# Layer-norm sums moved from TensorE to GpSimd in an RWKV block, with the raw weights on SyncE's queue

## The chip, the cores and the metric

The kernel runs on one core of one Trainium2 chip. The metric is device time in microseconds (us) of one execution; lower is better. A core has TensorE (PE, matrix products into the PSUM memory), VectorE (DVE), ScalarE (ACT), GpSimd (POOL) and SyncE (SP). Each engine takes its own instructions in order, and they wait for each other through semaphores. PE reads its operands from SBUF; DVE and ACT read SBUF or PSUM; GpSimd works on SBUF. Transfers (DMAs) are issued from the queues of SP, ACT and POOL.

## The reference

The input x has shape (2, 4096, 256): 2 sequences, 4096 time steps, 256 features.

```python
def _layernorm(x, axis=-1, eps=1e-05):
    m = jnp.mean(x, axis=axis, keepdims=True)
    v = jnp.var(x, axis=axis, keepdims=True)
    return (x - m) / jnp.sqrt(v + eps)

x = x + attention(_layernorm(x))
x = x + ffn(_layernorm(x))
```

The attention mixes each normalised time step with the one before it by three vectors, takes three products with 256x256 weights (k, v and r), runs a recurrence over time (a running log-maximum and a numerator with exponentials, the "wkv" scan), multiplies by sigmoid(r), and takes a product with W_o. The feed-forward part (ffn) takes two products from 256 to 1024 (w1, w2; silu of one times the other), two from 1024 to 1024 (h1, h2; gelu after each), and one back from 1024 to 256 (w3), each with a scale per output.

## The kernel before

Features lie on the 128 partitions and time along the free dimension; 256 features are two chunks. The work is cut into 16 tiles of 512 time steps, 8 for each sequence. A layer norm therefore sums across partitions.

**Products.** The ffn works in a split form: each operand is a pair (hi, lo), where hi is the value rounded to a shorter format (fp32r) and lo the remainder in the same format, and each product is two matmuls (`split_product`, lines 174 and 175). The attention's products are plain fp32 (`product`, line 167). After a product of the hidden layers ACT writes hi (L592) and the unrounded `full` (L594), and DVE subtracts them to give lo (L595). The next layer's products read both.

**The check of the weights.** The ffn's weights are kept as rounded copies. `compare` loads a raw piece of 128x512 values through GpSimd's queue (L154), and DVE compares it with the kept piece and counts differences (L156). There are 44 pieces: 28 of w1, w2, h1 and w3, and 16 of h2, which are compared while a block of h2 lies in SBUF. Where a difference is found, a second form of the whole block (`general_block`) runs after this one.

**The layer norm before.** `average` (lines 184 to 204) forms a mean over 256 features. DVE adds the two chunks (`both`, L189). ACT moves the upper 64 partitions down (`folded`, L191), DVE adds the lower 64 (L194), ACT rounds the result (`parts`, L196), and DVE puts the remainder into the other 64 partitions (L199). Then one matmul with a matrix of 1/256 sums over the partitions and gives the mean to every partition (L203). `layernorm` uses it twice: for the mean (then two subtractions, L214, and ACT's squares, L217) and for the variance (then ACT's square root, L220, DVE's reciprocal, L222, and two multiplications, L224).

**The order of the work.** The first tile has code of its own (`first_tile`), written out in order by `on`, `behind` and `last`. Then a loop runs `ffn(i)` as a generator of 26 steps (8 for w1 and w2, 8 for h1, 8 for h2, 2 for w3). Between its steps it takes pieces of two other generators: `attention(i + 1)`, which ends with the norm of x2 for the next ffn, and `normalise(i + 2)`, the first norm of the tile after. The piece of work at a step gives a scheduler its priorities; the scheduler then sets each engine's order, and an engine with nothing urgent that is ready is given later work (the mix operations, L304 and L305, of a later tile). `tc.issue_after` puts an instruction behind a named one.

**Buffers and queues.** The h2 blocks come from a copy in HBM through SP's queue (L588), three ahead. GpSimd's queue carries x in, the results out (L616), the raw pieces, and in the opening the rounding loads of the weights and the copies of h2 (L125). `ps_ffn` has four PSUM banks and `full` three buffers.

Of the kernel before, what the change touches and what calls it, by code (L numbers as in the profile page):

```python
# [2 lines left out]

# [4 lines left out]

F32 = mybir.dt.float32
# [56 lines left out]
def split_block(ctx, tc, flags, x, vecs, w_attn, w1, w2, h1, h2, w3, out):  # L66


    nc = tc.nc
    tensor, vector, scalar = nc.tensor, nc.vector, nc.scalar  # L70
# [61 lines left out]
    eps = const.tile([P, 1], F32, name="eps")  # L132
# [8 lines left out]
    numer = const.tile([P, ND], F32, name="numer")  # L141


    pieces = []
    for sb, src in ((w1_sb, w1), (w2_sb, w2), (h1_sb, h1), (w3_sb, w3)):
        n = src.shape[1] * src.shape[2] // PIECE
        sb, src = (t.rearrange("p a b -> p (a b)") for t in (sb, src))
        pieces += [(sb[:, k * PIECE : (k + 1) * PIECE], src[:, k * PIECE : (k + 1) * PIECE]) for k in range(n)]
    rounded = const.tile([P, len(pieces) + NH * (NH * P // PIECE)], F32, name="rounded")
    found = iter(range(rounded.shape[1]))  # L150

    def compare(kept, given, shape):
        raw = tmp.tile(shape, F32, tag="full", name="raw")
        nc.gpsimd.dma_start(out=raw, in_=given)  # L154
        j = next(found)
        vector.scalar_tensor_tensor(  # L156
            raw, raw, 1.0, kept.bitcast(F32), ALU.mult, ALU.not_equal, accum_out=rounded[:, j : j + 1]
        )

    def col(base, j):  # L160
        return vec[:, base + j : base + j + 1]
# [19 lines left out]
        marks["rounded"] = scalar.activation(hi, full, AF.Copy)  # L181
        marks["rest"] = vector.tensor_tensor(lo, full, hi.bitcast(F32), ALU.subtract)  # L182

    def average(a, b, tag, name, pause=False):

        both = one.tile([P, TS], F32, tag=tag, name="both")
        marks["both"] = vector.tensor_tensor(both, a, b, ALU.add)  # L189
        folded = one.tile([P // 2, TS], F32, tag="folded", name="folded")  # L190
        marks["shift"] = scalar.activation(folded, both[P // 2 :, :], AF.Copy)  # L191
        if pause:
            yield
        marks["fold"] = vector.tensor_tensor(folded, folded, both[: P // 2, :], ALU.add)  # L194
        parts = one.tile([P, TS], F32R, tag="parts", name="parts")
        marks["hi"] = scalar.activation(parts[: P // 2, :], folded, AF.Copy)  # L196
        if pause:
            yield
        marks["split"] = vector.tensor_tensor(parts[P // 2 :, :], folded, parts[: P // 2, :].bitcast(F32), ALU.subtract)  # L199
        if pause:  # L200
            yield
        psum = ps_sum.tile([P, TS], F32, tag="ps", name=name)
        marks["average"] = tensor.matmul(psum, mean_wr, parts, start=True, stop=True)  # L203
        return psum

    def layernorm(src, new_xc, tag, pause=False):


        mean = yield from average(src[:, 0, :], src[:, 1, :], tag, "mean", pause)
        if pause:  # L210
            yield
        xc = new_xc()
        for h in range(ND):
            vector.tensor_tensor(xc[:, h, :], src[:, h, :], mean, ALU.subtract)  # L214
        yield
# [5 lines left out]
        yield  # L221
# [53 lines left out]
    def normalise(i):  # L275

        x_sb = loaded.pop(i)
        if i + 1 < len(tiles):
            loaded[i + 1] = load_x(i + 1)
        xn = []  # L280

        def new_xn():

            xn.append(one.tile([P, ND, TS + 1], F32, tag="xn", name="xn"))
            if tiles[i][1] == 0:
                vector.memset(xn[0][:, :, 0:1], 0.0)
            else:
                vector.tensor_copy(xn[0][:, :, 0:1], prev)
            return xn[0][:, :, 1:]

        yield from layernorm(x_sb, new_xn, "rstd1", pause=i == 1)
        vector.tensor_copy(prev, xn[0][:, :, TS:])
        normal[i] = (x_sb, xn[0])

# [47 lines left out]
    def on(engine, operation, *args, **kwargs):  # L342
        with behind(engine):
            last[engine] = getattr(getattr(nc, engine), operation)(*args, **kwargs)  # L344
# [56 lines left out]
    def first_tile(second):  # L401
# [126 lines left out]
        last["vector"], last["scalar"] = marks["both"], marks["shift"]  # L528
# [35 lines left out]

    def ffn(i, x1, x2):

        checks = pieces[2 * (i - 1) : 2 * i] if i > 0 else []
        ha = []
        for f in range(NH):
            fs = slice(f * P, (f + 1) * P)  # L570
# [11 lines left out]
        for layer, scales in enumerate((SH1, SH2)):  # L582
            src, ha = ha, []
            for f in range(NH):
                fs = slice(f * P, (f + 1) * P)
                if layer == 1:
                    block = stream.tile([P, NH, P], F32R, tag="h2", name="h2_sb")
                    nc.sync.dma_start(out=block.bitcast(F32), in_=h2_hbm[f].bitcast(F32))  # L588
# [5 lines left out]
                scalar.activation(full, ps, AF.Gelu, scale=col(scales, f))  # L594
                vector.tensor_tensor(lo, full, hi.bitcast(F32), ALU.subtract)  # L595
                ha.append((hi, lo))
                if layer == 0 and f % 4 == 0 and checks:
                    compare(*checks.pop(), [P, PIECE])
                if layer == 1 and i == f + 1:
                    n = PIECE // P  # L600
                    for c in range(0, NH, n):
                        compare(block[:, c : c + n, :], h2[:, c : c + n, fs], [P, n, P])
                yield
        for h in range(ND):
            ps = ps_ffn.tile([P, TS], F32, tag="pf", name="po")
# [12 lines left out]
    def run(steps):  # L618
        for _ in steps:
            pass  # L620
# [8 lines left out]
        vector.tensor_scalar(inexact, everywhere, 0.0, None, ALU.is_gt)  # L629
        return inexact  # L630

    assert len(pieces) <= 2 * (len(tiles) - 1)
    normal, got = {}, {}
    second = normalise(1)
    first_tile(second)
# [2 lines left out]
    for i in range(len(tiles)):  # L638
        ahead = attention(i + 1) if i + 1 < len(tiles) else iter(())
        further = normalise(i + 2) if i + 2 < len(tiles) else iter(())  # L640
        for step, _ in enumerate(ffn(i, *got.pop(i))):
            if i == 0:
                if step in (0, 1, 2, 3, NH - 1):
                    with tc.issue_after(marks["rounded"].ins), tc.issue_after(marks["rest"].ins):
# [12 lines left out]
    return inexact[0:1, 0:1]  # L657


# [275 lines left out]
```

## Time and profile before

| What | Value |
|---|---|
| median of 3 runs | 1566.05 us (1565.85 to 1567.45) |
| the profiled execution's own time | 1567.88 us |
| its span | 1566.0 us |
| mean granted TensorE clock | 0.998 |
| one steady tile (332.2 to 427.9 us) | 95.7 us: PE busy 95.7, DVE 70.7, ACT 65.4, POOL 4.1 |

A row of a group reads: line, engine, operation, output<-inputs, sizes, count | busy us in total, mean ns of one | idle time of the engine just before, and what ended most of it. A row of the timeline reads: start us, duration us, engine, line, operation, and in brackets idle time before. Matmuls are pipelined and their ends are modelled, so the distance from start to start tells more of them than the duration does. GpSimd's spans are rough.

### The profile page before, as it was taken

The numbers are of one execution on the slowest core, as the hardware profiler recorded it, in microseconds if no ns is written. First come the engines' busy times: TensorE is split into PE (matmuls) and PEld (weight loads), VectorE is DVE, ScalarE is ACT, GpSimd is POOL, SyncE is SP. The second block draws the span as 40 slices with busy tenths as digits, with TensorE's granted clock in tenths as the row PEclk, the third lists the DMA queues.
The fourth block names the chain that finished last, engine by engine and source line by source line (L and its number), as shares of the span: only waits on it lengthen the run. The fifth ranks groups of instructions, "written<-read, shape, count | busy, mean of one in ns | idle before, by whom it ended". The sixth has DMA issues, their size and how long they took to land.

```text
span 1566.0 us, 16640 instructions
## 1 busy us (share of the span) xinstructions
PE 1555.8 (99%) x6313; PEld 1182.9 (76%) x6313; DVE 1102.0 (70%) x1763; ACT 1035.9 (66%) x1395; POOL 62.7 (4%) x100
## 2 busy tenths in 40 slices
PE   9999999999999999999999999999999999999998
PEld 6768777777777778777787777877777777777886
DVE  6788686776768767787676867767677676865531
ACT  5686757767577585776757766675776757756542
POOL 3000000000000000000000000000000000000000
PEclk9999999999999999999999999999999999999999
DMA  8612031120302204022030311203112030110302
GB/s 268 136 41 95 14 121 41 68 87 15 127 28 80 75 21 134 15 82 73 34 122 14 105 50 48 94 14 108 39 56 88 12 117 28 67 61 21 108 0 83
DMA packets 36886, 109.16 MB, mean 70 GB/s; under 512 B 3712, under 2 KB 12672, under 8 KB 36288
## 3 DMA queue, kind: packets, MB, share of 16 engines
q1 hardware_dynamic: 19424, 68.32, 13.1%
q0 software_dynamic: 16816, 39.07, 8.1%
q8 instruction: 51, 0.84, 0.2%
q10 hardware_dynamic: 560, 0.66, 0.1%
q14 instruction: 35, 0.29, 0.1%
HBM read 99.64 MB, written 12.58 MB: 72 GB/s over the span
## 4 chain that ended last, share of the span: by engine, by line
PE 98%; DVE 1%; ACT 0%; issue 0%; DVEq 0%
PE ph L174 30%; PE ph L175 30%; PE pa L174 4%; PE pb L174 4%; PE pb L175 4%; PE pa L175 4%; PE po L175 4%; PE po L174 4%; PE ps_k L167 3%; PE ps_r L167 3%; PE ps_v L167 3%; PE ps_o L167 3%; PE mean L203 1%; PE var L203 1%; PE ps_k L344 1%; DVE scale L344 0%
## 5 line engine op out<-in xcount | busy, mean ns | idle before, releaser
L174 PE MATMUL ph<-hi,h_sb 128*128 128x512 f32 x2048 | 813.5, 397 | 0.0
L175 PE MATMUL ph<-lo,h_sb 128*128 128x512 f32 x2048 | 801.0, 391 | 0.0
L174 PEld LDWEIGHTS ph<-hi,h_sb 128*128 128x128 f32 x2048 | 384.7, 188 | 93.5 <-issue 11.7
L175 PEld LDWEIGHTS ph<-lo,h_sb 128*128 128x128 f32 x2048 | 384.7, 188 | 89.1 <-issue 8.4
L592 ACT ACTIVATE hi<-ph,vec 128x512 fp32r<-128x512 f32 x256 | 175.7, 686 | 186.0 <-PE ph L175 184.5
L595 DVE TENSOR_TENSOR lo<-full,hi 128x512 fp32r<-128x512 f32 x256 | 175.5, 686 | 173.3 <-ACT full L594 172.2
L594 ACT ACTIVATE full<-ph,vec 128x512 f32<-128x512 f32 x256 | 174.3, 681 | 0.8 <-DVE lo L595 0.8
L577 DVE SCALAR_TENSOR_TENSOR gated<-pb,vec,gated 128x512 f32<-128x512 f32 x128 | 95.6, 748 | 57.6 <-PE pb L175 31.8
L592 ACT ACT_TABLE_LOAD x102 | 130.9, 1283 | 1.8
L576 ACT ACTIVATE gated<-pa,vec 128x512 f32<-128x512 f32 x128 | 86.6, 684 | 61.5 <-PE pa L175 58.3
L222 DVE RECIPROCAL rstd<-rstd 128x512 f32<-128x512 f32 x30 | 100.4, 3346 | 5.5 <-ACT rstd L220 5.5
L174 PE MATMUL pa<-x_hi,w_sb 128*128 128x512 f32 x256 | 101.9, 398 | 0.1
L174 PE MATMUL pb<-x_hi,w_sb 128*128 128x512 f32 x256 | 101.8, 398 | 0.0
L175 PE MATMUL pb<-x_lo,w_sb 128*128 128x512 f32 x256 | 100.6, 393 | 0.0
L175 PE MATMUL pa<-x_lo,w_sb 128*128 128x512 f32 x256 | 100.6, 393 | 0.0
L175 PE MATMUL po<-lo,w_sb 128*128 128x512 f32 x256 | 100.2, 392 | 0.0
L174 PE MATMUL po<-hi,w_sb 128*128 128x512 f32 x256 | 100.0, 391 | 0.0
L181 ACT ACTIVATE hi<-gated 128x512 fp32r<-128x512 f32 x128 | 80.6, 630 | 25.3 <-DVE gated L577 23.9
L182 DVE TENSOR_TENSOR lo<-gated,hi 128x512 fp32r<-128x512 f32 x128 | 87.8, 686 | 4.8 <-ACT hi L181 0.2
L250 DVE TENSOR_TENSOR_SCAN lm<-vec,lm,ps_k 128x512 f32<-128x512 f32 x30 | 38.3, 1278 | 44.2 <-PE ps_k L167 44.1
L305 DVE SCALAR_TENSOR_TENSOR mx<-xn,vec,mx 128x512 f32<-128x512 f32 x90 | 66.5, 745 | 0.3
L607 DVE SCALAR_TENSOR_TENSOR x_sb<-po,vec,x_sb 128x512 f32<-128x512 f32 x32 | 24.0, 751 | 59.0 <-PE po L175 59.0
(147 smaller groups left out, 1810.7 us busy)
## 6 DMA issues: line engine op xcount, KB each, us to landing
h_sb<-h_hbm SPq DMA_DIRECT2D x128, 512.0 KB, 3.2
raw<-in_h POOLq DMA_DIRECT2D x32, 256.0 KB, 3.1
x_sb<-in_x POOLq DMA_DIRECT2D x15, 512.0 KB, 4.0
out<-x_sb POOLq DMA_DIRECT2D x15, 512.0 KB, 3.1
h_sb<-in_h POOLq DMA_DIRECT2D x1, 4096.0 KB, 20.2
h_hbm<-in_h POOLq DMA_DIRECT2D x8, 512.0 KB, 12.7
w_sb<-in_w POOLq DMA_DIRECT2D x3, 1024.0 KB, 11.0
raw<-in_w POOLq DMA_DIRECT2D x12, 256.0 KB, 2.8
```

What stands on the lines that cost most here:

```text
L167: tensor.matmul(psum, weights(c), src[c], start=c == 0, stop=c == n - 1)
L174: tensor.matmul(psum, weights(c), hi, start=c == 0, stop=False)
L175: tensor.matmul(psum, weights(c), lo, start=False, stop=c == n - 1)
L181: marks["rounded"] = scalar.activation(hi, full, AF.Copy)
L182: marks["rest"] = vector.tensor_tensor(lo, full, hi.bitcast(F32), ALU.subtract)
L222: vector.reciprocal(rstd, rstd)
L305: vector.scalar_tensor_tensor(mx[:, h, :], xn[:, h, 1:], vec[:, j : j + 1], mx[:, h, :], ALU.mult, ALU.add)
L576: scalar.activation(full, pa, AF.Silu, scale=col(S1, f))
L577: vector.scalar_tensor_tensor(full, pb, col(S2, f), full, ALU.mult, ALU.mult)
L592: scalar.activation(hi, ps, AF.Gelu, scale=col(scales, f))
L594: scalar.activation(full, ps, AF.Gelu, scale=col(scales, f))
L595: vector.tensor_tensor(lo, full, hi.bitcast(F32), ALU.subtract)
```

## The change

- `average` becomes `total`: DVE adds the two chunks as before, and one GpSimd instruction, `partition_all_reduce`, sums over the 128 partitions and writes the sum to all of them, in SBUF. The folding, the rounding and the matmul go. The division by 256 moves into the subtraction and into the scale of the square root.
- The first norm's pieces are cut anew: sum; subtraction, squares and sum; square root, reciprocal and multiplications. These pieces (steps 12, 14 and 16) and the compares are issued after the latest hi, full and lo (`in_turn`). For tile 1 the pieces stand at steps 1 and 6 in place of 0, 1, 2, 3 and 7.
- A small `partition_all_reduce` in the opening makes GpSimd fetch the instruction's code there. A small add at the end, behind the last sum, brings back the usual code.
- Raw pieces are fetched through SP's queue, behind the latest h2 block, into one buffer, three steps before their compare; three pieces a tile, at steps 12, 16 and 20. The pieces of h2 are rounded again by ACT instead of being compared with the block in SBUF.

```diff
-    def average(a, b, tag, name, pause=False):
+    @contextmanager
+    def in_turn():
+        with tc.issue_after(marks["rounded"].ins), tc.issue_after(marks["rest"].ins):
+            yield
+
+    def total(a, b, tag):
         both = one.tile([P, TS], F32, tag=tag, name="both")
         marks["both"] = vector.tensor_tensor(both, a, b, ALU.add)
-        folded = one.tile([P // 2, TS], F32, tag="folded", name="folded")
-        marks["shift"] = scalar.activation(folded, both[P // 2 :, :], AF.Copy)
...
-        marks["fold"] = vector.tensor_tensor(folded, folded, both[: P // 2, :], ALU.add)
-        parts = one.tile([P, TS], F32R, tag="parts", name="parts")
-        marks["hi"] = scalar.activation(parts[: P // 2, :], folded, AF.Copy)
...
-        marks["split"] = vector.tensor_tensor(parts[P // 2 :, :], folded, parts[: P // 2, :].bitcast(F32), ALU.subtract)
...
-        psum = ps_sum.tile([P, TS], F32, tag="ps", name=name)
-        marks["average"] = tensor.matmul(psum, mean_wr, parts, start=True, stop=True)
-        return psum
+        everywhere = one.tile([P, TS], F32, tag="total", name="total")
+        marks["sum"] = nc.gpsimd.partition_all_reduce(everywhere, both, channels=P, reduce_op=ReduceOp.add)
+        return everywhere
...
-    def layernorm(src, new_xc, tag, pause=False):
-        mean = yield from average(src[:, 0, :], src[:, 1, :], tag, "mean", pause)
-        if pause:
+    def layernorm(src, new_xc, tag, spread=False):
+        mean = total(src[:, 0, :], src[:, 1, :], tag)
+        if spread:
             yield
         xc = new_xc()
         for h in range(ND):
-            vector.tensor_tensor(xc[:, h, :], src[:, h, :], mean, ALU.subtract)
-        yield
+            vector.scalar_tensor_tensor(xc[:, h, :], mean, -1.0 / D, src[:, h, :], ALU.mult, ALU.add)
+        if not spread:
+            yield
         sq = wide.tile([P, ND, TS], F32, tag="wide", name="sq")
         scalar.activation(sq, xc, AF.Square)
-        var = yield from average(sq[:, 0, :], sq[:, 1, :], tag, "var")
+        var = total(sq[:, 0, :], sq[:, 1, :], tag)
+        if spread:
+            yield
         rstd = one.tile([P, TS], F32, tag=tag, name="rstd")
-        scalar.activation(rstd, var, AF.Sqrt, bias=eps)
-        yield
+        scalar.activation(rstd, var, AF.Sqrt, bias=eps, scale=1.0 / D)
+        if not spread:
+            yield
         vector.reciprocal(rstd, rstd)
...
+    def fetch(j):
+        fetched[j] = stream.tile([P, PIECE], F32, tag="raw", name="raw", bufs=1)
+        with tc.issue_after(marks["block"].ins):
+            nc.sync.dma_start(out=fetched[j], in_=pieces[j][1])
+
+    def compare(j):
+        raw, kept = fetched.pop(j), pieces[j][0]
+        with in_turn():
+            if kept is None:
+                kept = tmp.tile([P, PIECE], F32R, tag="full", name="kept")
+                scalar.activation(kept, raw, AF.Copy)
+            vector.scalar_tensor_tensor(
+                raw, raw, 1.0, kept.bitcast(F32), ALU.mult, ALU.not_equal, accum_out=rounded[:, j : j + 1]
+            )
...
         load_table(AF.Exp)
         on("gpsimd", "tensor_copy", prev, xn[:, :, TS - 1 :])
+        on("gpsimd", "partition_all_reduce", root, eps, channels=P, reduce_op=ReduceOp.add)
...
+    steps = (NH + 4, 2 * NH, 2 * NH + 4)
...
             if step > 2 * NH - 6 and step % 2 == 0:
-                next(further, None)
+                with in_turn():
+                    next(further, None)
+            for k, at in enumerate(steps if i > 0 else ()):
+                j = (i - 1) * len(steps) + k
+                if j < len(pieces) and step in (at - 3, at):
+                    (fetch if step < at else compare)(j)
...
+    with tc.issue_after(marks["sum"].ins):
+        nc.gpsimd.tensor_tensor(root, eps, eps, ALU.add)
```

More of the change, by code (lines that the diff above doesn't have):

```diff
@@ L1 @@
 import math
-from contextlib import ExitStack, nullcontext
+from contextlib import ExitStack, contextmanager, nullcontext
 import concourse.bass as bass
@@ L7 @@
 from concourse._compat import with_exitstack
+from concourse.bass_isa import ReduceOp
 F32 = mybir.dt.float32
@@ L144, in split_block @@
     pieces = []
-    for sb, src in ((w1_sb, w1), (w2_sb, w2), (h1_sb, h1), (w3_sb, w3)):
+    for sb, src in ((w1_sb, w1), (w2_sb, w2), (h1_sb, h1), (w3_sb, w3), (None, h2)):
         n = src.shape[1] * src.shape[2] // PIECE
[L147 to L158, printed above, removed]
+        sb, src = (t if t is None else t.rearrange("p a b -> p (a b)") for t in (sb, src))
+        for k in range(n):
+            ks = slice(k * PIECE, (k + 1) * PIECE)
+            pieces.append((None if sb is None else sb[:, ks], src[:, ks]))
+    rounded = const.tile([P, len(pieces)], F32, name="rounded")
+    fetched = {}
+    def fetch(j):
[11 more added lines that the diff above has]
+            )
     def col(base, j):
@@ L182, in split @@
         marks["rest"] = vector.tensor_tensor(lo, full, hi.bitcast(F32), ALU.subtract)
-    def average(a, b, tag, name, pause=False):
+    @contextmanager
[3 more added lines that the diff above has]
+    def total(a, b, tag):
         both = one.tile([P, TS], F32, tag=tag, name="both")
         marks["both"] = vector.tensor_tensor(both, a, b, ALU.add)
-        folded = one.tile([P // 2, TS], F32, tag="folded", name="folded")
-        marks["shift"] = scalar.activation(folded, both[P // 2 :, :], AF.Copy)
-        if pause:
-            yield
-        marks["fold"] = vector.tensor_tensor(folded, folded, both[: P // 2, :], ALU.add)
-        parts = one.tile([P, TS], F32R, tag="parts", name="parts")
-        marks["hi"] = scalar.activation(parts[: P // 2, :], folded, AF.Copy)
-        if pause:
-            yield
-        marks["split"] = vector.tensor_tensor(parts[P // 2 :, :], folded, parts[: P // 2, :].bitcast(F32), ALU.subtract)
-        if pause:
-            yield
-        psum = ps_sum.tile([P, TS], F32, tag="ps", name=name)
-        marks["average"] = tensor.matmul(psum, mean_wr, parts, start=True, stop=True)
-        return psum
-    def layernorm(src, new_xc, tag, pause=False):
-        mean = yield from average(src[:, 0, :], src[:, 1, :], tag, "mean", pause)
-        if pause:
+        everywhere = one.tile([P, TS], F32, tag="total", name="total")
[4 more added lines that the diff above has]
+        if spread:
             yield
@@ L213, in layernorm @@
         for h in range(ND):
-            vector.tensor_tensor(xc[:, h, :], src[:, h, :], mean, ALU.subtract)
-        yield
+            vector.scalar_tensor_tensor(xc[:, h, :], mean, -1.0 / D, src[:, h, :], ALU.mult, ALU.add)
+        if not spread:
+            yield
         sq = wide.tile([P, ND, TS], F32, tag="wide", name="sq")
         scalar.activation(sq, xc, AF.Square)
-        var = yield from average(sq[:, 0, :], sq[:, 1, :], tag, "var")
+        var = total(sq[:, 0, :], sq[:, 1, :], tag)
+        if spread:
+            yield
         rstd = one.tile([P, TS], F32, tag=tag, name="rstd")
-        scalar.activation(rstd, var, AF.Sqrt, bias=eps)
-        yield
+        scalar.activation(rstd, var, AF.Sqrt, bias=eps, scale=1.0 / D)
+        if not spread:
+            yield
         vector.reciprocal(rstd, rstd)
@@ L289, in new_xn @@
             return xn[0][:, :, 1:]
-        yield from layernorm(x_sb, new_xn, "rstd1", pause=i == 1)
+        yield from layernorm(x_sb, new_xn, "rstd1", spread=True)
         vector.tensor_copy(prev, xn[0][:, :, TS:])
@@ L527, in first_tile @@
             next(second)
-        last["vector"], last["scalar"] = marks["both"], marks["shift"]
+        last["vector"] = marks["both"]
         banks = [
@@ L565, in ffn @@
     def ffn(i, x1, x2):
-        checks = pieces[2 * (i - 1) : 2 * i] if i > 0 else []
         ha = []
@@ L587, in ffn @@
                     block = stream.tile([P, NH, P], F32R, tag="h2", name="h2_sb")
-                    nc.sync.dma_start(out=block.bitcast(F32), in_=h2_hbm[f].bitcast(F32))
+                    marks["block"] = nc.sync.dma_start(out=block.bitcast(F32), in_=h2_hbm[f].bitcast(F32))
                 ps = ps_ffn.tile([P, TS], F32, tag="pf", name="ph")
@@ L593, in ffn @@
                 full = tmp.tile([P, TS], F32, tag="full", name="full")
-                scalar.activation(full, ps, AF.Gelu, scale=col(scales, f))
-                vector.tensor_tensor(lo, full, hi.bitcast(F32), ALU.subtract)
+                marks["rounded"] = scalar.activation(full, ps, AF.Gelu, scale=col(scales, f))
+                marks["rest"] = vector.tensor_tensor(lo, full, hi.bitcast(F32), ALU.subtract)
                 ha.append((hi, lo))
[L597 to L602, printed above, removed]
                 yield
@@ L630, in any_inexact @@
         return inexact
-    assert len(pieces) <= 2 * (len(tiles) - 1)
+    steps = (NH + 4, 2 * NH, 2 * NH + 4)
+    assert len(pieces) <= len(steps) * (len(tiles) - 1)
     normal, got = {}, {}
@@ L642, in split_block @@
             if i == 0:
-                if step in (0, 1, 2, 3, NH - 1):
-                    with tc.issue_after(marks["rounded"].ins), tc.issue_after(marks["rest"].ins):
+                if step in (1, NH - 2):
+                    with in_turn():
                         next(second)
@@ L651, in split_block @@
             if step > 2 * NH - 6 and step % 2 == 0:
-                next(further, None)
+                with in_turn():
+                    next(further, None)
[3 more added lines that the diff above has]
+                    (fetch if step < at else compare)(j)
             if i == len(tiles) - 1 and step == 3 * NH - 2:
```

## The prediction

> **What bounds the kernel now.** I read the page first (busy times, the chain that ended last), then the groups by line, then the timeline of PE and DVE around one norm. On the page:
>
> ```profile
> PE 1555.8 (99%) x6313; PEld 1182.9 (76%) x6313; DVE 1102.0 (70%) x1763; ACT 1035.9 (66%) x1395; POOL 62.7 (4%) x100
> ...
> PE 98%; DVE 1%; ACT 0%; issue 0%; DVEq 0%
> ```
>
> TensorE is busy everywhere and carries the chain. Its longest gap is 2 us in the opening. So only two things move the end: fewer slots on PE, or something that makes PE wait. A share of 70% on DVE is worth nothing by itself, but DVE is in order and hands PE its operands, so its order decides whether PE waits. The groups that the change touches:
>
> ```profile
> L203 PE MATMUL mean<-parts,mean_wr 128*128 128x512 f32 x30 | 18.5, 616 | 0.1
> L203 PE MATMUL var<-parts,mean_wr 128*128 128x512 f32 x30 | 17.9, 597 | 0.0
> L199 DVE TENSOR_TENSOR parts<-folded,parts 64x512 fp32r<-64x512 f32 x60 | 41.1, 685 | 31.0 <-ACT parts L196 30.1
> L194 DVE TENSOR_TENSOR folded<-folded,both 64x512 f32<-64x512 f32 x60 | 40.6, 678 | 1.4 <-ACT folded L191 1.4
> ...
> L344 POOL TENSOR_TENSOR mx<-mx 128x511 f32<-128x511 f32 x2 | 2.5, 1267 | 8.7 <-ACT mx L344 8.7
> ```
>
> Durations of matmuls overlap, so a matmul's price is read from starts. PE's timeline at the norm of x2, and after fp32 products with and without a sum between:
>
> ```profile
> 593.76 0.39 PE L174 MATMUL ph<-hi,h_sb 128*128 128x512 f32 x1
> 594.12 0.50 PE L203 MATMUL mean<-parts,mean_wr 128*128 128x512 f32 x1
> 594.46 0.40 PE L175 MATMUL ph<-lo,h_sb 128*128 128x512 f32 x1
> 594.70 0.39 PE L174 MATMUL ph<-hi,h_sb 128*128 128x512 f32 x1
> ```
>
> ```profile
> 565.72 0.79 PE L203 MATMUL mean<-parts,mean_wr 128*128 128x512 f32 x1
> 566.35 0.39 PE L174 MATMUL ph<-hi,h_sb 128*128 128x512 f32 x1
> ...
> 1426.88 0.79 PE L174 MATMUL ph<-hi,h_sb 128*128 128x512 f32 x1
> 1427.51 0.39 PE L175 MATMUL ph<-lo,h_sb 128*128 128x512 f32 x1
> ```
>
> The ordinary pitch is 0.23 us. The mean of x2 makes 0.36 + 0.34 = 0.70 us where one pitch would stand: 0.47 us. The mean of the first norm comes right after fp32 products; the 0.63 us behind it stands at 1426.88 too, where no sum is, so it belongs to the products and only one pitch, 0.23 us, is the sum's.
>
> **The change part by part.**
>
> *PE loses 60 matmuls.* A middle tile has four: 0.47 (mean of x2), about 0.26 (variance of x2, from its two gaps less a pitch), 0.23 and 0.23 (first norm). That is 1.2 us a tile, 15 norm pairs: **18 us**, all on the path.
>
> *DVE and ACT lose the folding.* DVE: L194 and L199, 41 + 41 = 82 us. ACT: L191 and L196, 120 copies of 0.63 us, 75 us. Neither is on the path; this is only room. Added: ACT rounds 16 pieces of h2 again (about 0.65 us each, 10 us), hidden by the ACT time freed. The mean's subtraction becomes a scalar_tensor_tensor, 0.75 for 0.68 us, 60 times, 4 us, hidden likewise. The 44 compares stay, three a tile instead of four in eight tiles and two in the rest.
>
> *Raw weights on SP.* 44 fetches of 256 KB with a landing of about 3 us, issued three steps (3.6 us each) before their compare: nothing. A fetch waits for the compare of the piece before (one buffer) and the h2 blocks queue behind it on SP; blocks are fetched three ahead, 11 us, and that compare stands at least one step earlier. Cover gone, a late compare would hold the block and so PE.
>
> *The opening.* POOL gets the code fetch and a dummy sum before its log_max and numer copies; these ended at 30.2 us because of DVE, the preceding copy at 16.0, so some 14 us are free; the Trainium skill (GPSIMD Engine Reference, Instruction dispatch) has about 6 us for a first call, and no row here shows one. The first real sum sits between the first and the other seven h2 copies, which so start after about 34 us plus a sum instead of 31.6. The first h2 block is asked for at 40.1, but products use it only from about 100 us. Nothing, if a sum is under some 20 us. At the end POOL's extra add and code switch lie beside the last 100 us of products: nothing. POOL also issues the out and x transfers; they stand behind the tile's last sum and start at the tile's end anyway.
>
> *The sums themselves.* 60 sums over partitions of 128x512 on POOL: nothing in the trace shows one. From below: the one 128x511 elementwise row, 1.27 us, which reads and writes the same tile without crossing partitions. From above: the Trainium skill (GPSIMD Engine Reference, Cross-partition) measured 247.7 us for a partition-axis reduce of [128, 2048]; a quarter is 62 us, an estimate, for a different instruction. At 62 us POOL alone would need 60 x 62 = 3720 us. I take 2.5 us, twice the near row, because a sum has to carry values between partitions and back where that row only streams them; call it X. Both ends stay in the range of cases below.
>
> What must cover X is DVE's work between the add (`both`) and the first use, in the built order, with DVE's pitches (0.6 for a 128x512 two-input operation, 0.65 with a scalar, 0.4 tensor_scalar, 3.3 reciprocal):
> - mean of the first norm: consumed two steps later, over 7 us.
> - variance of the first norm: the x_sb adds (waiting on products), a lo, a compare, a both, about 4.0; less the sqrt of 0.7: X up to 3.3.
> - mean of x2: reciprocal, lo, two multiplies: 3.3 + 0.6 + 1.2 = 5.1.
> - variance of x2: lo and five mix operations, 3.4, less sqrt and its hand-over 0.8: X up to 2.6.
>
> Behind each wait on DVE stand the next `lo` subtractions, and behind sqrt on ACT the next hi and full; `lo` is what PE's products read. Its slack now:
>
> ```profile
> 419.44 1.22 DVE L182 TENSOR_TENSOR x_lo<-x,x_hi 128x1024 fp32r<-128x1024 f32 x1
> 420.60 0.69 DVE L595 TENSOR_TENSOR lo<-full,hi 128x512 fp32r<-128x512 f32 x1
> ```
>
> ```profile
> 422.53 0.39 PE L175 MATMUL po<-lo,w_sb 128*128 128x512 f32 x1
> ...
> 426.43 0.39 PE L174 MATMUL pa<-x_hi,w_sb 128*128 128x512 f32 x1
> ```
>
> The last lo of a tile is ready at 421.3 and read at 422.5: 1.2 us. (x_lo, at 420.7, is read by the next tile from 426.4: 5.8 us.) So PE loses per tile (X - 3.3) + (X - 2.6) + (X - 5.1), each if positive, less 1.2. At X = 2.5 that is nothing; it starts at X = 3.6; it eats the gain of 1.2 us at 4.1; from there an extra us costs 30 and later 45 us of the whole. Sum at 2.5: 1567.9 (the profiled execution's own time; 1566.0 span) - 18 = 1549.9. That execution is 1.8 above the median 1566.05, so 1548 on the median's scale; I give **1549**.
>
> *The rule that speaks against it.* Row first: the two POOL rows of 1.27 us ran at 13.4 to 15.9 us beside DVE operations that read one operand from PSUM, and neither shows a delay; no row has POOL reading beside a two-input DVE operation. The Trainium skill (SBUF — State Buffer, Who interferes with whom) says that just this pair excludes each other: DVE with two SBUF inputs and a GpSimd instruction that reads SBUF share one interface, and the second waits until the first is done. Then the cover named above doesn't run: the lo, mix, compare and multiply operations have two SBUF inputs. What runs is the reciprocal and the PSUM adds. Per tile: (X - 1.6) + (X - 3.3) + X - 1.2, where positive. At X = 2.5: 0.9 + 0 + 2.5 - 1.2 = 2.2 us, 15 times 33 us, less 18: 1567.9 + 15 = 1583. So 1549 without the rule, 1583 with it, both at the same X; with it the gain survives only below X = 2.0. Whether this custom instruction holds the interface for its whole length or in short reads no run here shows; I put that at less than even.
>
> **The rivals.**
> 1. *The port lock* (slower). Place: DVE's lo and mix operations after the x2 variance add; price as above: X = 2: 1568; 2.5: 1583; 3: 1598; 4: about 1637. It decides from X = 2.0. For it: the rule; 66 us of DVE work a tile of 96. Against: no row.
> 2. *A long sum, no lock* (slower). Place: DVE's reciprocal of x2, which waits for sqrt, which waits for POOL. X = 5: (1.7 + 2.4 - 1.2) x 15 = 43, less 18: 1593; 6: 87 - 18: 1637; 10: about 1810. It decides from 4.1. For it: a sum across partitions does more per column than the 1.27 us row, and the other end is 62; against: nothing measured.
> 3. *Even.* The slots go and the waits give just that back: X near 4.1 without the lock or 2.0 with it: 1563 to 1569.
> 4. *The change doesn't free what it says*: if every gap after L203 belonged to the products, 60 x 0.23 = 14 us, 1554; still faster.
>
> **How the numbers follow.** A difference of 0.2%, 3 us, is about what a measurement here can tell from none. My case (18 us gained, a little given back, rival 4 included) 0.48, its own range 1545 to 1562; even 0.06; the lock 0.26; a long sum 0.20. Faster 0.48, same 0.06, slower 0.46. Below 1545 I see 3 in 100: nothing else leaves PE. Above, 1640 takes in the lock up to X = 4 and a long sum up to 6; beyond are some 15 in 100. Range 1545 to 1640.
>
> **What would show it.** Right: no L203 on PE, a period of 94.5 us a tile for 95.7, POOL rows of the sum near 2.5 us, DVE's reciprocal idle under 1 us before it, PE idle as before. The lock: lo and mix rows that start just when a sum ends, or rows as long as the sum. A long sum: reciprocal and subtraction idle with POOL or ACT rstd as releaser, PE idle before po with DVE lo as releaser, 4 gaps a tile. Code fetch: log_max copies late. Raw fetch: PE waiting for the DMA of an h2 block. If POOL's sum is over 4 us, or PE shows idle time in every tile, the forecast is wrong.

## The result and the profile after

The changed kernel takes 1571.28 us, the median of 8 runs (1569.6 to 1571.78); the kernel before, on the same chip, 1566.21 us. The ratio is 1.0029, with a 95% interval of 1.0018 to 1.004: slower by 0.3%, where 1549 was forecast, with a range of 1545 to 1640. The profiled execution took 1570.13 us, its span is 1568.3, and the granted clock was 1.0.

The page of the changed kernel, first its busy times and the chain that ended last, then groups by line (busy us, mean ns | idle before, releaser):

```profile
PE 1542.8 (98%) x6253; PEld 1171.0 (75%) x6253; DVE 1068.3 (68%) x1643; ACT 1030.7 (66%) x1334; POOL 238.6 (15%) x118
...
PE 69%; DVE 25%; ACT 4%; POOL 1%; issue 1%; POOLq 0%
...
L206 POOL PARTITION_ALL_REDUCE total<-both x60 | 202.0, 3367 | 920.1 <-DVE both L204 908.8
L603 DVE TENSOR_TENSOR lo<-full,hi 128x512 fp32r<-128x512 f32 x256 | 182.0, 712 | 193.1 <-ACT full L602 193.1
...
L186 PE MATMUL po<-lo,w_sb 128*128 128x512 f32 x256 | 103.7, 405 | 15.4 <-DVE lo L603 15.4
...
L312 DVE SCALAR_TENSOR_TENSOR mx<-xn,vec,mx 128x512 f32<-128x512 f32 x90 | 86.2, 982 | 0.0
```

TensorE has 60 matmuls fewer and is busy 13.0 us less, but the chain is no longer PE's alone: a quarter runs through DVE. PE now waits in front of `po` for `lo`. A mix operation (L312), which took 745 ns before, takes 982 ns on average. A sum takes 3.4 us on average.

The period, from the start of a tile's first `ps_k` to the next in PE's timeline, went from some 95.7 us to 96.4 in nine periods in a row and 95.5 in the last four (the one before these, next to the opening, is shorter in both kernels). Without the sums' matmuls it should have been 94.5. So about 2 us a tile are lost in most tiles. The timelines of GpSimd, DVE and PE in one of them (start, duration) show where:

```profile
489.72 3.23 POOL L206 PARTITION_ALL_REDUCE total<-both  x1 [18.00 <-DVE both L204]
493.89 3.23 POOL L206 PARTITION_ALL_REDUCE total<-both  x1 [0.94 <-DVE both L204]
502.94 3.53 POOL L206 PARTITION_ALL_REDUCE total<-both  x1 [5.82 <-DVE both L204]
```

```profile
491.35 1.16 DVE L603 TENSOR_TENSOR lo<-full,hi 128x512 fp32r<-128x512 f32 x1 [1.07 <-ACT full L602]
...
493.75 3.35 DVE L229 RECIPROCAL rstd<-rstd 128x512 f32<-128x512 f32 x1
...
503.30 2.73 DVE L312 SCALAR_TENSOR_TENSOR mx<-xn,vec,mx 128x512 f32<-128x512 f32 x1
505.95 1.19 DVE L311 TENSOR_SCALAR mx<-xn,unmix 128x512 f32<-128x512 f32 x2
507.06 1.40 DVE L312 SCALAR_TENSOR_TENSOR mx<-xn,vec,mx 128x512 f32<-128x512 f32 x2
508.39 3.34 DVE L229 RECIPROCAL rstd<-rstd 128x512 f32<-128x512 f32 x1
...
518.46 0.68 DVE L603 TENSOR_TENSOR lo<-full,hi 128x512 fp32r<-128x512 f32 x1
```

```profile
516.63 0.40 PE L185 MATMUL po<-hi,w_sb 128*128 128x512 f32 x1
517.27 0.50 PE L186 MATMUL po<-lo,w_sb 128*128 128x512 f32 x1 [0.24 <-DVE lo L603]
517.61 0.40 PE L185 MATMUL po<-hi,w_sb 128*128 128x512 f32 x1
519.20 0.50 PE L186 MATMUL po<-lo,w_sb 128*128 128x512 f32 x1 [1.19 <-DVE lo L603]
519.53 0.39 PE L185 MATMUL po<-hi,w_sb 128*128 128x512 f32 x1
```

The row of ACT that takes the result of the third sum:

```profile
506.50 0.73 ACT L226 ACTIVATE rstd<-total,eps 128x512 f32<-128x512 f32 x1 [3.41 <-POOL total L206]
```

The first two sums are those of the first norm's variance and of x2's mean; the third is x2's variance. Beside the third a mix operation takes 2.73 us, 2.0 more than its usual 0.74, and the pair of L311 behind it 1.19 for 0.87; beside the first a `lo` takes 1.16 for 0.69. The reciprocal that runs beside the second keeps its 3.35. After 491.35 DVE has no idle time until its last `lo`, so these delays stay in its queue: mix, mix, reciprocal, each later, and the last `lo` is done at 519.14. PE's four distances from 516.63 to 519.53 make 0.64 + 0.34 + 1.59 + 0.33 = 2.90 us where four pitches of 0.23 us make 0.92: 1.98 us lost, which is 96.4 - 94.4.

Three theories remain open at this point. The sum's reading of SBUF holds DVE up (the port lock: the two engines share a way into SBUF, and the second waits for the first). Or the sum is simply long, and what waits for it is late. Or DVE has too much in this window, mixes and comparisons ahead of the last `lo`, whatever GpSimd does.

### The profile page after: what moved, and what is told of

It reads as the page before. It is cut to its first block, busy times and chain, and to the rows that moved or that the text cites. A ratio compares the mean times of both kernels' runs of the same rounds, so it can differ in the third digit from the quotient of the medians.

```text
span 1568.3 us, 16558 instructions
## 1 busy us (share of the span) xinstructions
PE 1542.8 (98%) x6253; PEld 1171.0 (75%) x6253; DVE 1068.3 (68%) x1643; ACT 1030.7 (66%) x1334; POOL 238.6 (15%) x118
## 4 chain that ended last, share of the span: by engine, by line
PE 69%; DVE 25%; ACT 4%; POOL 1%; issue 1%; POOLq 0%
PE ph L185 18%; PE ph L186 18%; DVE rstd L229 6%; DVE mx L312 5%; DVE lo L603 4%; PE pa L185 4%; PE pb L185 4%; PE pa L186 4%; PE pb L186 4%; PE ps_k L178 3%; PE ps_v L178 3%; PE ps_r L178 3%; PE ps_o L178 3%; DVE mx L311 3%; PE po L186 3%; PE po L185 2%
## 5 line engine op out<-in xcount | busy, mean ns | idle before, releaser
L185 PE MATMUL ph<-hi,h_sb 128*128 128x512 f32 x2048 | 823.0, 402 | 0.6 <-ACT hi L192 0.6
L186 PE MATMUL ph<-lo,h_sb 128*128 128x512 f32 x2048 | 810.1, 397 | 0.0
L206 POOL PARTITION_ALL_REDUCE total<-both x60 | 202.0, 3367 | 920.1 <-DVE both L204 908.8
L603 DVE TENSOR_TENSOR lo<-full,hi 128x512 fp32r<-128x512 f32 x256 | 182.0, 712 | 193.1 <-ACT full L602 193.1
L186 PE MATMUL po<-lo,w_sb 128*128 128x512 f32 x256 | 103.7, 405 | 15.4 <-DVE lo L603 15.4
L312 DVE SCALAR_TENSOR_TENSOR mx<-xn,vec,mx 128x512 f32<-128x512 f32 x90 | 86.2, 982 | 0.0
L186 PEld LDWEIGHTS po<-lo,w_sb 128*128 128x128 f32 x256 | 48.0, 188 | 37.8 <-DVE lo L603 28.3
```

Of the source, the lines that this page charges most:

```text
L185: tensor.matmul(psum, weights(c), hi, start=c == 0, stop=False)
L186: tensor.matmul(psum, weights(c), lo, start=False, stop=c == n - 1)
L206: marks["sum"] = nc.gpsimd.partition_all_reduce(everywhere, both, channels=P, reduce_op=ReduceOp.add)
L312: vector.scalar_tensor_tensor(mx[:, h, :], xn[:, h, 1:], vec[:, j : j + 1], mx[:, h, :], ALU.mult, ALU.add)
```

## The experiments

All twelve were timed against the kernel before, whose median was between 1566.0 and 1566.8 us.

| Kernel | Median us | Ratio to before (95%) | Period of the middle tiles |
|---|---|---|---|
| sums that nobody reads, added to the kernel before | 1618.79 | 1.0333 (1.0319 to 1.0347) | 99.0 |
| one memset for each sum | 1545.98 | 0.987 (0.9855 to 0.9885) | 94.4 |
| six memsets for each sum | 1546.96 | 0.9876 (0.9861 to 0.9891) | 94.4 |
| three ordinary additions for each sum | 1574.38 | 1.0048 (1.0034 to 1.0061) | 95.7, later 98.6 |
| sum over half the columns | 1549.85 | 0.9895 (0.9879 to 0.991) | 94.6 |
| mixes moved | 1547.05 | 0.9875 (0.986 to 0.989) | 94.4 |
| comparisons moved | 1565.21 | 0.9993 (0.9985 to 1.0001) | 95.7 |
| both moved | 1548.01 | 0.9884 (0.9869 to 0.9899) | 94.4 |
| mixes moved in the kernel before | 1570.05 | 1.0023 (1.0016 to 1.003) | 96.0 |
| x2's variance back on TensorE | 1562.44 | 0.9971 (0.9961 to 0.9981) | 95.2 |
| the same, both moved | 1562.81 | 0.9976 (0.9968 to 0.9985) | 94.9 |
| both sums of x2 back, both moved | 1569.96 | 1.0028 (1.0018 to 1.0039) | 95.7 |

**Sums that nobody reads.**

```diff
         var = yield from average(sq[:, 0, :], sq[:, 1, :], tag, "var")
+        marks["sum"] = nc.gpsimd.partition_all_reduce(sq[:, 0, :], sq[:, 1, :], channels=P, reduce_op=ReduceOp.add)
```

> The kernel before, unchanged in its own sums over the channels, with 30 GpSimd sums of 128x512 added that nobody reads: one half of each squared tile is summed over the partitions into the other half, which is dead by then (two sums a tile, at the place of the two variances; the small one that fetches the code in the opening and the small addition at the end are there too). So the latency of the sum is on no path; only what it does to VectorE's access to SBUF can cost. Port lock: VectorE's lo or mix operations beside a sum grow by about 2 us each, the last lo before po is late in part of the tiles, and the time is 1570 to 1580 for 1566.2. Latency of the sum, or its place in VectorE's order: 1566 to 1567, and the lo and mix rows keep their 686 and 745 ns.

It took 1618.79 us, 52 us more than before and far more than I had expected of any theory. Its timelines of GpSimd, DVE and PE, and PE's waits (total us, times, longest):

```profile
397.53 3.23 POOL L220 PARTITION_ALL_REDUCE sq<-sq  x1 [19.66 <-DVE both L190]
```

```profile
397.82 2.50 DVE L598 TENSOR_TENSOR lo<-full,hi 128x512 fp32r<-128x512 f32 x1 [0.46 <-ACT full L597]
```

```profile
398.93 0.39 PE L175 MATMUL ph<-hi,h_sb 128*128 128x512 f32 x1
400.37 0.51 PE L176 MATMUL ph<-lo,h_sb 128*128 128x512 f32 x1 [1.05 <-DVE lo L598]
```

```profile
PE var L204 <- DVE parts L200: 27.8, 17, 1.9
PE ph L176 <- DVE lo L598: 14.0, 13, 1.4
```

Nothing depends on these sums, and no other engine waits for GpSimd's work in this trace; still a `lo` beside one takes 2.5 us and PE waits for it. The sum acts on DVE by being there, not by its result. In this kernel each blocked operation stands just ahead of what PE needs next: `lo` of the running product, and `parts`, for which the matmul of the variance waits in PE's own queue. PE's waits in the two rows make 41.8 of the 52 us; the kernel before has neither. So the same 2 us cost more here than in the changed kernel.

**Writes in place of the sum.** One memset, then six, which are as long as the sum (the edit of the six; the other has no loop):

```diff
-        marks["sum"] = nc.gpsimd.partition_all_reduce(everywhere, both, channels=P, reduce_op=ReduceOp.add)
+        for _ in range(6):
+            marks["sum"] = nc.gpsimd.memset(everywhere, 100.0)
```

> The changed kernel with each GpSimd sum replaced by one GpSimd memset of the 128x512 result: the sum itself is left out, so the norms are wrong, while every other instruction, TensorE's 60 matmuls fewer among them, is that of the changed kernel. Port lock or latency: the whole loss is the sum's, PE idle before po goes below 2 us in all, and the time is 1549 to 1553 for 1571.3. Backlog: if the compares and mix operations placed ahead of the last lo make it late by themselves, the time stays above 1560 with lo as PE's releaser before po.

> The changed kernel with each sum replaced by six GpSimd memsets of its 128x512 result, together about as long as the sum (some 3 us) but reading nothing: the sum is left out, the norms are wrong, its latency stays. Port lock by the sum's reading: no lo or mix row is prolonged and the time is that of the single memset, within 3 us (1549 to 1555). Latency: the time stays at 1567 to 1571, with reciprocal and subtraction late as in the changed kernel. If the memsets hold VectorE up as well, rows of 2 us and more show it, and the run cannot tell the two apart.

1545.98 and 1546.96 us, 3 and 2 us below the ranges given: without the sum's reading the whole loss is gone. The kernel with six memsets, its chain and groups:

```profile
PE 98%; DVE 1%; ACT 0%; issue 0%
...
L207 POOL MEMSET total<- 128x512 f32 x360 | 194.5, 540 | 972.1 <-DVE xn L218 771.6
```

```profile
L313 DVE SCALAR_TENSOR_TENSOR mx<-xn,vec,mx 128x512 f32<-128x512 f32 x90 | 65.3, 736 | 0.0
```

Six of 0.54 us are 3.2 us for each sum (3.4 to 3.6 from start to end in the timeline), and the mix keeps its 736 ns. Writes of the sum's length don't hold up the operations that its reading holds up. But memsets read nothing, so they don't wait for `both` either. At x2's variance they start 2.5 us before it:

```profile
491.38 3.61 POOL L207 MEMSET total<- 128x512 f32 x6 [2.94 <-DVE x L218]
```

```profile
493.86 0.67 DVE L204 TENSOR_TENSOR both<-sq 128x512 f32<-128x512 f32 x1
```

So this kernel doesn't keep the wait for the result, as its expectation had it, and doesn't decide on the second theory. The changed kernel's trace does more for that. At the place shown, the square root is done at 507.23 and DVE comes to the reciprocal at 508.39 without idle time: it doesn't wait for the sum. In the whole execution DVE waits 4.0 us for the square root and 3.4 for a sum. ACT waits 45.3 us for sums, 3.41 of them here, but DVE has no idle time behind it, so no `lo` was late for that. What the length alone would have cost there is an estimate: without the delays of 2.0 and 0.3 us DVE would have come at some 506.1, and without its own 0.3 us the sum would have let the square root end at 506.9, so 0.9 us would have shown.

How much of a delay DVE can bear, the kernel with one memset shows. From the `lo` behind DVE's idle time to the last `lo` of the tile, its DVE has the same operations as the changed kernel's, a mix and a pair of L311 in another place, and PE's order is the same. The last `lo` and the matmul that reads it:

```profile
507.61 0.69 DVE L603 TENSOR_TENSOR lo<-full,hi 128x512 fp32r<-128x512 f32 x1
```

```profile
509.13 0.39 PE L186 MATMUL po<-lo,w_sb 128*128 128x512 f32 x1
```

The `lo` is done 0.8 us before it is read. DVE takes 25.1 us for the stretch here and 27.8 in the changed kernel: 2.7 more, less 0.8, is 1.9, about what PE loses. So mixes and comparisons ahead of the last `lo` cost nothing by themselves, which ends the third theory alone, and the estimated 0.9 us of length would have gone nearly whole into the slack. By this reckoning the blocking is nearly all of the loss. (With six memsets DVE's order differs more: the last two mixes stand behind the last `lo`.)

**Ordinary reads in place of the sum.**

```diff
-        marks["sum"] = nc.gpsimd.partition_all_reduce(everywhere, both, channels=P, reduce_op=ReduceOp.add)
+        for _ in range(3):
+            marks["sum"] = nc.gpsimd.tensor_tensor(everywhere, both, both, ALU.add)
```

> The changed kernel with each sum replaced by three ordinary GpSimd additions of its input to itself, each reading the 128x512 tile and writing the result, about 1.27 us each by the row of 128x511, 3.8 us together; the sum over the partitions is left out, so the norms are wrong. It asks whether reading SBUF is enough, or whether it is the special instruction that holds VectorE up. Reading: mix operations of 1.5 to 4 us beside these rows, PE waiting before po for lo, 1562 to 1580. The special instruction alone: no row is prolonged, and the time is that of the writes, 1545 to 1550.

1574.38 us, and ordinary reading is enough to hold DVE up. The rows of GpSimd and DVE at x2's variance:

```profile
500.45 3.78 POOL L207 TENSOR_TENSOR total<-both 128x512 f32<-128x512 f32 x3 [5.00 <-DVE both L204]
```

```profile
501.81 1.52 DVE L313 SCALAR_TENSOR_TENSOR mx<-xn,vec,mx 128x512 f32<-128x512 f32 x1
503.25 1.52 DVE L604 TENSOR_TENSOR lo<-full,hi 128x512 fp32r<-128x512 f32 x1
```

A mix and a `lo` take 1.52 us here, 0.8 more than usual and less than one addition (1142 ns on average): DVE gets in between the additions, as if the two engines took turns. The three additions take 3.78 us here and 3.27 beside a reciprocal. The time itself proves less than the rows, since PE's order differs in some places too: 1.3 us a tile are lost in the middle (95.7 - 94.4) and 4.2 in the last tiles. Why more there stays open.

**Half of the columns.**

```diff
-        marks["sum"] = nc.gpsimd.partition_all_reduce(everywhere, both, channels=P, reduce_op=ReduceOp.add)
-        return everywhere
+        half = TS // 2
+        marks["sum"] = nc.gpsimd.partition_all_reduce(
+            everywhere[:, :half], both[:, :half], channels=P, reduce_op=ReduceOp.add
+        )
+        return everywhere[:, :half].unsqueeze(1).to_broadcast([P, 2, half])
...
```

> The changed kernel with each GpSimd sum taken over 256 of the 512 columns and used for both halves, so the second half of each norm is wrong; VectorE and ScalarE still work on all 512 columns. The sum is shorter (1.6 to 2.0 us by half of 3.24 and a start). Port lock in proportion to what is read: the blocked lo and mix rows fall from 2.5 to 2.9 us to 1.5 to 1.8, about half of the 24.6 us between the changed kernel (1571.3) and the one with writes only (1547.0) goes: 1555 to 1563. A fixed price for each sum whatever it reads: 1568 to 1571, rows as long as before.

1549.85 us: some 3 of the 24 us stay (1546.96 with writes only), where I had expected half, and the range that I gave is missed. At x2's variance, GpSimd and DVE:

```profile
496.70 2.09 POOL L207 PARTITION_ALL_REDUCE total<-both  x1 [7.34 <-DVE both L204]
```

```profile
497.05 1.59 DVE L319 SCALAR_TENSOR_TENSOR mx<-xn,vec,mx 128x512 f32<-128x512 f32 x1
```

The mix loses 0.85 us instead of 2.0, in proportion as expected, but PE then loses only 0.2 us a tile (94.6 - 94.4). The first part of a delay is taken up by the slack of the last `lo` (0.8 us with one memset); only what exceeds it reaches PE. The sum is also shorter here, so this run alone doesn't divide the gain between the two.

**Moving what stands beside the sum.** All sums stay on GpSimd. The mixes of the next tile go from the window of the x2 norm to the first steps of the next pass; the comparisons go to earlier steps.

```diff
+            if i > 0 and step in (1, 3, 5):
+                with in_turn():
+                    next(ahead, None)
-            for _ in range(0 if step < NH else 4 if step == NH + (i == 0) else 1):
+            for _ in range(0 if step < NH else 4 if i == 0 and step == NH + 1 else 1):
                 next(ahead, None)
```

```diff
-    steps = (NH + 4, 2 * NH, 2 * NH + 4)
+    steps = (4, NH, NH + 4)
```

> The changed kernel with only the three mix pieces of the next tile moved out of the window of the x2 norm, to product steps 1, 3 and 5 of the next pass; the comparisons stay at steps 12, 16 and 20. The mixes are 12 operations, 7.4 us, of the window's filler, and it is they that are prolonged to 2.7 to 2.9 us beside the sum of x2's variance; the two comparisons there are 1.2 us. If the mixes are what makes the lock cost: a period of 94.4 to 94.7 and 1547 to 1553, near the run with both moves (1548.0). If the comparisons matter as much: 1555 to 1565.

> The changed kernel with only the comparisons moved, to product steps 4, 8 and 12; the mix pieces stay in the window of the x2 norm. If the mixes are what makes the lock cost, little is won: VectorE has 1.2 us less to do ahead of the last lo, so PE's wait before po (1.4 us a tile at most) shrinks but mixes of 2.7 us remain: 1558 to 1570. If the comparisons are the cause: 1547 to 1555.

> The changed kernel, all four sums of a tile on GpSimd, with the filler moved out of the window of the x2 norm: the three mix pieces of the next tile's inputs at product steps 1, 3 and 5 of the next pass, the comparisons at steps 4, 8 and 12. The lock then meets only lo operations there, one a product step of 7.2 us, with nothing in VectorE's queue between them but the norm. Lock plus backlog: a lo grows by 2 us, but the last lo before po has that much room: PE's idle time before po falls below 5 us (43.7 in the changed kernel over matmuls and weight loads), the period to 94.4 to 94.8 and the time to 1547 to 1554. Lock whatever stands there: a blocked lo makes PE wait in any case: 1562 to 1571. Mixing late could make ps_k wait for mx in the next pass; then PE shows that, 1555 to 1575.

1547.05 us with the mixes moved, 1565.21 with the comparisons moved, 1548.01 with both. The mixes are what makes the lock cost: moved alone, they win back all of it, and the changed kernel becomes 1.25% faster than the one before. The comparisons ahead of the last `lo` are worth 6 us as long as the mixes stand there, and nothing after. With the mixes moved, GpSimd and DVE at x2's variance, and the chain:

```profile
496.43 3.53 POOL L206 PARTITION_ALL_REDUCE total<-both  x1 [4.98 <-DVE both L204]
```

```profile
496.18 0.69 DVE L603 TENSOR_TENSOR lo<-full,hi 128x512 fp32r<-128x512 f32 x1
500.75 3.35 DVE L229 RECIPROCAL rstd<-rstd 128x512 f32<-128x512 f32 x1 [3.89 <-ACT rstd L226]
```

```profile
PE 98%; DVE 1%; ACT 1%; issue 0%
```

The sum now lies beside nothing but the end of a `lo`. DVE stands idle for 3.89 us while it and the square root run, which looks worse in a share of busy time, and the end comes 24 us earlier. The lock is still there: `lo` takes 722 ns on average, where 682 is its mean without reads. It has just nothing queued behind it that is short of time.

**The move alone.** The same three steps in the kernel before, whose sums stay on TensorE.

> The kernel before with the move of the three mix pieces alone (product steps 1, 3 and 5 of the next pass), its sums on TensorE as they were. If the move is worth something by itself, it is faster than 1566: down to 1560, by L203's matmuls waiting less for the folding. If it is only a cure for the lock: 1565 to 1568, or slower where the folding of x2, with no filler between, is no longer the limit but the matmuls' place in PE's order is: up to 1580.

1570.05 us, 0.2% slower than before. So the move is no gain of its own, as the second reading had it, and slightly worse; it is the cure of what the sums on GpSimd bring.

**Sums given back to TensorE.** x2's variance as before, then with both moves, then both sums of x2 with both moves. The edit of the first, which also brings back `average`:

```diff
-        var = total(sq[:, 0, :], sq[:, 1, :], tag)
         if spread:
-            yield
+            var = total(sq[:, 0, :], sq[:, 1, :], tag)
+            yield
+        else:
+            var = average(sq[:, 0, :], sq[:, 1, :], tag, "var")
...
```

> The changed kernel with the variance of x2 alone summed as before (two copies on ScalarE, two operations on VectorE and one matmul L203 a tile); the other three sums stay on GpSimd. Port lock: this sum stands beside the lo and mix operations of the last product steps, so most of PE's idle time before po (28 us by its weight loads) goes, against about 15 x 0.3 = 4.5 us of matmul that come back: 1553 to 1560. Latency: the path from the squares to the reciprocal was 2.6 us of folding for 3.2 us of sum, so at most 0.6 us a tile can go, less the matmul: 1566 to 1572. Backlog: the two folding operations put 1.1 us more on VectorE ahead of the last lo: 1572 to 1585.

> The same move of filler, with the variance of x2 summed as before on ScalarE, VectorE and TensorE (one matmul L203 a tile more, 0.23 to 0.47 us). Lock plus backlog: the matmul comes back and the last sum in the window is gone: a period of 94.7 to 95.0, 1551 to 1557, not better than all four sums on GpSimd without the filler. If lo operations blocked by the sums are still late there, it is the faster of the two, by 5 us or more.

> The same move of filler, with both sums of x2 as before (two matmuls L203 a tile more) and only the two sums of the norm two tiles ahead on GpSimd. If the sums of x2 are the whole of the loss and their latency or lock is unavoidable: the fastest of these three, at 1553 to 1557. If the filler was needed to make the lock hurt: slower than all four on GpSimd by two matmuls a tile, 15 x 0.46 = 7 us, at 1554 to 1561, and VectorE's folding for it stands in the window too.

1562.44, 1562.81 and 1569.96 us. The first regains 8.8 us on the changed kernel, 2.4 us short of the range that I gave for the lock; PE's weight loads before `po` wait 1.7 us for `lo` in all, for 28.3 in the changed kernel, but 12.0 before the new matmul for `parts`. It also takes away one sum's length, so it doesn't tell lock from length. The other two are 15 and 22 us slower than all four sums on GpSimd with both moves, more than expected. A matmul that is given back brings more than its slot, since it stands in PE's order and waits there for DVE's `parts`. PE's weight loads and matmuls in the second of these kernels:

```profile
PEld var L220 <- DVE parts L218: 11.1, 15, 3.3
...
PE var L220 <- DVE parts L218: 5.0, 5, 2.9
```

## Why the prediction was wrong

*PE bounds the kernel, and the 60 matmuls are worth 18 us: right, a little low.* With reads or mixes out of the way the period is 94.4 us (94.5 forecast), and the three such kernels take 1546 to 1547 us, 19 to 21 less than before.

*Raw weights on SP's queue, code fetch in the opening: nothing, as said.* Both are in the kernels of 1546 and 1547 us. The code fetch shows as 8.5 us without work ahead of GpSimd's small sum, in the free time named for it, and nothing waits for a raw piece.

*X = 2.5 us for a sum: too small, and nearly harmless.* Its rows are 3.23 us, and 3.53 where DVE holds it up at its start. The point from which length alone costs was put at 3.6. No run keeps the length and takes away only the reading; by the estimate above it costs about 0.1 us a tile. With the mixes moved, DVE waits 57.2 us in all for the square root behind the sums, 4.0 in the changed kernel, and the loss is gone all the same.

*The failed step is the judgment on the lock*: "Whether this custom instruction holds the interface for its whole length or in short reads no run here shows; I put that at less than even." It holds it for about two thirds of its length. The row in the changed kernel was 2.73 us for a mix of 0.74. The rule that the prediction set against the change (the Trainium skill, SBUF — State Buffer, Who interferes with whom) was the one to follow: reading by ordinary additions also holds up operations with two SBUF inputs, writing doesn't. The two rows of 1.27 us that I set against it had no two-input SBUF operation beside them and said nothing on the question; "no row" was no evidence for the other side.

*From this follows the second wrong step, the cover of x2's variance.* "Lo and five mix operations, 3.4" were counted as work that hides the sum. The `lo` and three of the five are two-input operations, and these are what the sum stops; at the same time they stand ahead of the reciprocal and the last `lo`. What was booked as cover was load. Moved away, it left nothing to stop.

*The rival's price was too high.* At the measured X = 3.24 its formula gives (3.24 - 1.6) + 0 + 3.24 - 1.2 = 3.7 us a tile and with 18 us of gain some 1605 us. PE lost 2.0 in most tiles and 1.1 in the last. For the third term, the sum stopped the mix by 2.0 us and not by X: counting back from the mix's end (503.30 + 2.73 - 0.74), it was free at 505.29, 2.35 us after the sum's start and 1.2 before its end. For the first term, the 1.64 us stood beside idle time of DVE, an operation on PSUM and a `lo` with 0.47 us of delay; the reciprocal behind it followed without a gap. And the slack of 1.2 us was 0.8 in the new order, as the kernel with one memset shows. That the end came within 0.3% of the time before is therefore no sign that nothing happened: about 19 us won and 24 lost. (Two prices of the rivals are a little low by their own formulas: 1638 for 1637 at X = 4, 1817 for 1810 at X = 10. Nothing hangs on them.)

## What to carry to other kernels

Before moving work to GpSimd, list which DVE operations will run beside it: here those with two SBUF inputs stopped while GpSimd read, and a tensor_scalar too, while a reciprocal went on. Work that an engine in order does "meanwhile" is cover only if it can run meanwhile and nothing urgent is queued behind it; otherwise place it elsewhere, even if the engine then stands idle. And test a suspected lock from both sides: add reads that nobody waits for, and replace the reader with writes of the same length. Tie the writes behind the operation whose result was read, or they start early, as the six memsets did, and the wait for the result goes together with the collision.

## What the runs showed of the hardware

- A sum over 128 partitions of 128x512 float32 on GpSimd takes 3.23 us, over half of the columns 1.79 to 1.80: about 0.36 us and 1.43 us for each 256 columns.
- The blocked operation with two inputs was let go before the sum's row ended (2.35 us into 3.53, and 1.2 into 2.09 for half of the columns; GpSimd's rows are rough). The rule named in the prediction has the interface held for the whole instruction; for this sum the measured rows are shorter, and they decide.
- The lock works both ways: a sum that starts while a `lo` is running is 3.53 us instead of 3.23.
- A DVE operation with one SBUF input is stopped too where it is a tensor_scalar (0.48 us for 128x512), and by writes as well: L311 takes 479 ns on average with one memset and 544 with six. In a late tile of the changed kernel, beside the sum from 1272.60 to 1275.92, a pair that takes 0.87 us elsewhere took 2.86.

```profile
1272.36 2.86 DVE L311 TENSOR_SCALAR mx<-xn,unmix 128x512 f32<-128x512 f32 x2
```
